# A two-layer graph network: the order of the node strips and where the nodes are prepared

## The chip, the cores and the metric

The kernel runs on one NeuronCore of a Trainium2 chip. The metric is device time in microseconds (us) of one execution; several executions of the same kernel are given by their median. Engines are called by their names in the trace: PE (TensorE), DVE (VectorE), ACT (ScalarE), POOL (GpSimd) and SP (the queue that issues most DMAs). Nodes lie in 26 blocks of 128 (3,327 nodes and one of padding).

## What is computed

Two residual layers over 3,327 nodes with 64 features and a dense 0/1 adjacency matrix of 3,327 x 3,327. Layer 0 sums, for every pair of nodes, an attention weight times a hyperbolic logarithm map; layer 1 is a weighted sum in which the weight halves with each later neighbour. Cut to what matters:

```python
h = jnp.maximum(_layernorm(x, axis=-1), 0.0)
# layer 0, on h
c = 1.0 / r[0] ** 2
x_t = logmap0(h, c)                       # needs artanh of the norm, so logarithms
left, right = x_t @ w_att[:D, 0], x_t @ w_att[D:, 0]
adj_att = sigmoid(left[:, None] + right[None, :] + b_att[0]) * adj
x_local = logmap(h[:, None, :], h[None, :, :], c)        # for every pair i, j
support = jnp.einsum('ij,ijd->id', adj_att, x_local)
x = x + proj(expmap(h, support, c), c)
# layer 1
h = jnp.maximum(_layernorm(x, axis=-1), 0.0)
support = h @ weight
rank = jnp.cumsum(adj != 0, axis=1); deg = rank[:, -1:]
k = jnp.minimum(deg, 100.0); pos = rank - (deg - k)
w = (adj != 0) * jnp.where(pos > 0, 0.5 ** (k - pos), 0.0)
x = x + w @ support + bias
```

## The kernel before

**Pairs and rounds.** The nodes i are cut into four strips of 8, 8, 6 and 4 blocks (`STRIPS`, line 29). For each strip the kernel goes through all 26 blocks j from the last to the first. A round is one such j (two j in the last strip, where two tiles of 512 columns lie side by side): 26 rounds for each of the first two strips, 26 for the third, 13 for the last. In round n (lines 1145 to 1194) the engines do, on tiles of 128 x 1024:

- DVE, line 1169: the attention weight (a tanh from ACT) times the adjacency tile `ad`. This line opens a round on DVE.
- DVE, line 626 (`edges`): the 0/1 mask of a later round's tile.
- PE, lines 637 and 638 (`count`): how many neighbours lie behind each pair, accumulated in PSUM; it is copied out by `read` (lines 641 to 652), in one round by ACT and in the next by DVE, into `behind_hi`, `weight_of` or `behind_lo`, for layer 1.
- ACT, line 659 (`sigmoids`): the tanh of left + right for the next round.
- PE, lines 666 and 667 (`products`): two matmuls of features, `ju` by `iu` and `jz` by `iz`, that give the pair's function argument in `pq`.
- ACT, lines 1162 and 1163: two Gelus on `pq`, in place.
- DVE, line 1186: `pq` times the weight; PE, line 676 (`total`): the sum over j with the table `hw`, two rounds later.

So a steady round holds on DVE 1169, 626, 1186 and every other time a read; on ACT two Gelus, a tanh and every other time a read. PE, DVE and ACT execute in the order in which the program is written (`manual_schedule`, line 685). SP and POOL take their work in an order that the framework chooses. `ad` has five buffers, `sg` five, `pq` two.

**Preparation, lines 689 to 884.** Before the first round the nodes' features have to be there: `x_sb` is loaded in two halves of 13 blocks, then for all 26 blocks at once: mean and centring (701, 702), squares and relu on ACT (703 to 705), sums (721, 723), a reciprocal root by a guess and three Newton steps on DVE (728), `x2`, `bal`, `babs`, `nrm`, `yz` (730 to 768). The scaled features `zf` are split into an f16 part and an f16 remainder (`nz`), and `nu` holds them with seven columns more. Blocks 0 to 7 (`first_i`) and 24, 25 (`last_j`) are turned by PE first and copied to `jz` and `ju`; four DMAs make from these the strip's `iz` and `iu` (`strip_in`, line 572), two of them issued on POOL for the first strip. Then logarithms for all blocks on ACT, with a table load before (801) and after (815), the artanh on DVE (818 to 822), and `logits`, which multiplies `jz` with the attention vectors into `left` and `right`. `first_left` transposes `left` for the first strip. The blocks 8 to 23 (`later`) follow: zf, rounding, transposes on PE in two groups, the second in `last_of_ahead` (line 853), a generator of which round 0 and round 1 take a piece each (lines 1187 to 1189; those rounds skip `advance`). It also makes `left_d` (left in DRAM, for the later strips), the table `hw`, and some columns for later. The adjacency tiles of rounds 0 and 1 are masked, counted and read before any of this is ready (706, 716 to 719).

**After the strips, lines 1202 to 1277.** Layer 1: the counts are turned into weights (`decode`), alternately by ACT and DVE, and PE adds up over j in the order: the four blocks of `JD` (12 to 15), then the other blocks of the first three strips, then the blocks of the last strip (`late`), whose `s2` is ready last. `close` writes out each 512 nodes.

**Post-processing of a strip** (`post`, line 930) runs during the next strip's rounds in small portions (`advance`), its small operations on POOL; these are the operations of line 982 in the trace, among them powers (`ALU.pow`) on 128 x 8.

## Time and profile before

| | us |
|---|---|
| median of 3 runs (425.24 to 426.3) | 426.22 |
| the profiled execution, its own time | 425.4 |
| its span, first to last instruction | 423.7 |
| busy: PE / DVE / ACT / POOL | 361.3 / 377.9 / 364.6 / 114.0 |

The profiled execution's own time is 1.7 us more than its span. In the page the span is cut into 40 slices of 10.6 us, and each digit is the busy share of an engine in tenths. Rows of a timeline give start, duration, engine, line, operation, output and inputs with their shapes, and in brackets how long the engine stood idle before and what released it. The chain of work that ended last consists, for 32% of the span, of DVE work, for 28% of ACT work and for 21% of PE work. The three costliest lines of the rounds on DVE and ACT are

| line | engine, what | count | mean, ns |
|---|---|---|---|
| 1186 | DVE, weight times pq | 91 | 1144 |
| 1169 | DVE, tanh times ad | 91 | 1145 |
| 659 | ACT, tanh | 103 | 978 |
| 1162, 1163 | ACT, Gelus | 90 each | 957, 946 |
| 626 | DVE, mask | 91 | 653 |

### The profile page before, as it was taken

To read this page: it belongs to the slowest core of one execution; us is meant where nothing else is said; L and a number is where in the kernel's file an instruction comes from. 1 tells how busy PE (TensorE), PEld (TensorE's weight loads), DVE (VectorE), ACT (ScalarE), POOL (GpSimd) and SP (SyncE) were. 2 spreads that over 40 slices of the span, in tenths; PEclk is the share of its full clock that TensorE was granted. 3 is DMA by queue.
4 is the path that set the end of the run, shared out by engine and by line. 5 is a ranking of instruction groups with operands and counts; after the bars stand their busy time and mean duration, and the time that the engine had idled before them with its cause. 6 is when DMAs were issued, how large, how long until landed. Compare 5 with 4: busy or idle time off the path is not lost.

```text
span 423.7 us, 4689 instructions
## 1 busy us (share of the span) xinstructions
PE 361.3 (85%) x1437; PEld 155.1 (37%) x1460; DVE 377.9 (89%) x557; ACT 364.6 (86%) x410; POOL 114.0 (27%) x218
## 2 busy tenths in 40 slices
PE   0246779999999899999999799999787999899693
PEld 0024323333333333333333444444332333244353
DVE  4886899999999999999999898899998999898841
ACT  3468859999999999999999999999898899789720
POOL 6010000000000044780061061940523375362400
PEclk9999989999999999999999899999998999999987
DMA  7311544545456535543444454444553430000012
GB/s 184 150 39 39 151 131 124 164 145 177 137 167 183 169 116 159 181 143 112 149 124 148 120 150 122 140 130 132 164 143 105 137 99 0 2 0 0 2 26 63
DMA packets 23248, 48.98 MB, mean 116 GB/s; under 512 B 8713, under 2 KB 9169, under 8 KB 23215
## 3 DMA queue, kind: packets, MB, share of 16 engines
q1 hardware_dynamic: 21087, 47.81, 38.3%
q10 hardware_dynamic: 1808, 0.46, 0.6%
q0 software_dynamic: 320, 0.33, 0.5%
q8 instruction: 13, 0.21, 0.2%
q14 instruction: 20, 0.16, 0.1%
HBM read 46.40 MB, written 0.87 MB: 112 GB/s over the span
## 4 chain that ended last, share of the span: by engine, by line
DVE 32%; ACT 28%; PE 21%; issue 12%; POOL 2%; DMA 2%; SPq 0%; POOLq 0%; DVEq 0%; ACTq 0%
ACT sg L659 9%; DVE sg L1186 8%; ACT pq L1162 8%; PE po L676 8%; DVE sg L1169 7%; DVE wt L1218 3%; ACT pq L1163 3%; ACT behind_lo L648 3%; PE pq L666 2%; DMA ad<-in_adj_t 2%; PE pq L667 2%; DVE behind_lo L652 2%; ACT behind_hi L648 2%; PE pc L638 2%; PE pc L637 2%
## 5 line engine op out<-in xcount | busy, mean ns | idle before, releaser
L676 PE MATMUL po<-sg,hw 128*65 128x512 f32 (+1 forms) x364 | 161.4, 567 | 0.9 <-DVE st L910 0.4
L1186 DVE SCALAR_TENSOR_TENSOR sg<-pq,sg 128x1024 f32<-128x1024 f32 (+1 forms) x91 | 104.1, 1144 | 6.8 <-ACT pq L1163 5.6
L1169 DVE SCALAR_TENSOR_TENSOR sg<-sg,ad 128x1024 f32<-128x1024 f32 (+1 forms) x91 | 104.2, 1145 | 1.6 <-ACT sg L659 1.4
L659 ACT ACTIVATE sg<-left_b,right 128x1024 f32<-128x1024 f32 (+2 forms) x103 | 99.4, 978 | 0.7 <-DVE right L834 0.7
L1162 ACT ACTIVATE pq<-pq 128x1024 f32<-128x1024 f32 (+1 forms) x90 | 86.1, 957 | 4.8 <-PE pq L667 4.6
L1163 ACT ACTIVATE pq<-pq 128x1024 f32<-128x1024 f32 (+1 forms) x90 | 85.2, 946 | 2.8
L676 PEld LDWEIGHTS po<-sg,hw 128*65 128x65 f32 x364 | 49.7, 139 | 71.5 <-issue 56.0
L637 PE MATMUL pc<-mask,ca 128*128 128x512 bf16 (+1 forms) x166 | 60.7, 366 | 15.6 <-DVE behind_hi L652 7.0
L638 PE MATMUL pc<-mask,cb 128*128 128x512 bf16 (+1 forms) x172 | 62.4, 372 | 12.9 <-DVE mask L626 10.6
L666 PE MATMUL pq<-iu,ju 71*128 71x512 f16 (+1 forms) x182 | 68.6, 377 | 1.7 <-DMA iu<-ju 0.7
L667 PE MATMUL pq<-iz,jz 128*128 128x512 f16 (+1 forms) x182 | 67.4, 377 | 0.9 <-DMA iz<-jz 0.9
L626 DVE TENSOR_SCALAR mask<-ad 128x1024 bf16<-128x1024 f32 (+1 forms) x91 | 59.5, 653 | 1.5 <-DMA ad<-in_adj_t 1.5
L638 PEld LDWEIGHTS <-cb 128*128 128x128 bf16 x182 | 17.9, 98 | 66.8 <-issue 49.0
L982 POOL TENSOR_TENSOR dots<-dots,ih 128x8 f32<-128x8 f32 (+1 forms) x3 | 2.6, 874 | 137.2 <-DVE dots L1002 137.2
L1230 PE MATMUL pw<-wt,s 128*128 128x512 bf16 (+1 forms) x151 | 33.7, 375 | 4.3 <-DVE s L1087 2.3
L637 PEld LDWEIGHTS <-ca 128*128 128x128 bf16 x175 | 17.4, 99 | 30.1 <-issue 18.4
L648 ACT ACTIVATE behind_hi<-pc 128x1024 uint8<-128x1024 f32 (+2 forms) x24 | 20.7, 863 | 7.0 <-PE pc L638 7.0
L1230 PEld LDWEIGHTS <-s 128*128 128x128 f16 x182 | 18.0, 101 | 23.6 <-issue 4.2
L666 PEld LDWEIGHTS <-ju 71*128 71x128 f16 x182 | 18.1, 99 | 23.3 <-DVE sg L1186 3.8
L667 PEld LDWEIGHTS <-jz 128*128 128x128 f16 x182 | 18.3, 100 | 21.2 <-issue 3.0
L648 ACT ACTIVATE behind_lo<-pc 128x1024 uint8<-128x1024 f32 (+2 forms) x29 | 24.9, 858 | 0.0
L1235 POOL TENSOR_TENSOR x_sb<-x_sb,bias_b 128x256 f32<-128x256 f32 (+1 forms) x6 | 10.0, 1673 | 49.5 <-DVE w L1071 44.0
(298 smaller groups left out, 365.7 us busy)
## 6 DMA issues: line engine op xcount, KB each, us to landing
ad<-in_adj_t SPq DMA_DIRECT2D x65, 512.0 KB, 3.6
ad<-in_adj_t SPq DMA_DIRECT2D x26, 384.0 KB, 3.1
out<-o SPq DMA_DIRECT2D x6, 128.0 KB, 1.9
left_b<-left_d SPq DMA_DIRECT2D x1, 512.0 KB, 4.7
x_sb<-in_x SPq DMA_DIRECT2D x1, 416.0 KB, 5.0
x_sb<-in_x ACTq DMA_DIRECT2D x1, 416.0 KB, 5.7
iz<-jz SPq DMA_DIRECT2D x3, 128.0 KB, 2.4
left_b<-left_d SPq DMA_DIRECT2D x1, 384.0 KB
```

What stands on the lines that cost most here:

```text
L626: V.tensor_scalar(*args, 0.0, None, op0=ALU.not_equal)
L637: T.matmul(S.pc[:, f0:f1], ca, S.before[:, f0:f1], start=False, stop=True, skip_group_check=True)
L638: T.matmul(S.pc[:, f0:f1], cb, now[:, f0:f1], start=S.first, stop=True, skip_group_check=True)
L648: A.activation(kept, S.pc[:, : S.F], AF.Relu, scale=128.0 if j in JD else 1.0)
L659: A.activation(part(n, sg, j), S.left[:, : S.F], AF.Tanh, bias=right[:, j : j + 1], scale=0.5)
L666: T.matmul(part(n, pq, j, f0, f1), ju[:KB, j, :], S.iu[:, f0:f1], start=True, stop=False)
L667: T.matmul(part(n, pq, j, f0, f1), jz[:, j, :], S.iz[:, f0:f1], start=False, stop=True)
L676: T.matmul(S.po[: D + 1, f0:f1], hw[:, j, :], part(n, sg_of[n], j, f0, f1), start=j == NB - 1, stop=j == 0)
L1162: A.activation(pq, pq, AF.Gelu, scale=-WG / QS)
L1163: A.activation(pq, pq, AF.Gelu, scale=WH)
L1169: V.scalar_tensor_tensor(sg, sg, 1.0, ad_of.pop(n)[:, :w], op0=ALU.add, op1=ALU.mult)
L1186: V.scalar_tensor_tensor(sg, pq, WD, sg, op0=ALU.add, op1=ALU.mult)
```

## The change

The strips are taken in the opposite order of nodes: blocks 18 to 25 first, then 10 to 17, 4 to 9, and 0 to 3 last. As j also runs from 25 down, the first strip's eight blocks are the j of its first eight rounds. Only these eight are prepared ahead of the rounds (`first`); the other 18 (`others`) are prepared in pieces by a generator, `second_group`, one piece at the end of each of the rounds 0 to 8.

Parts of this preparation change engine. For the first eight blocks the additional columns of nu and the table `hw` are made by POOL; `iz` and `iu` come from a second, swapped copy of the features (`nz1[:, 1]`, `nu1[:, 1]`) by two transposing DMAs on SP rather than from `jz` and `ju` by four plain ones. For the other 18 all columns of one value per node are made by POOL, with powers for the two roots and the reciprocal, and so is `hw`; `jz` and `ju` come by two transposing DMAs on SP rather than from PE with copies. The logarithms are taken twice, once for each group, with a table load before and after each. `nz2` and `nu2` use the memory of the two squares. `left_d` is written once for the 18 blocks by a DMA. In layer 1 the order of summation and the pieces of the bias follow the new strips.

Of rounds 0 and 1 the masks, counts and reads come later than before. New names that the text below uses: `the_rest` (POOL, eight operations), `clipped` (the argument of the logarithms), `logarithms` (ACT), `artanh` (DVE), `summing_table` (POOL, hw), `root_of` (POOL, a power and four operations).

```diff
-STRIPS = [(0, 8), (8, 8), (16, 6), (22, 4)]
+STRIPS = [(18, 8), (10, 8), (4, 6), (0, 4)]
...
-    node_halves = (slice(0, 13), slice(13, NB))
-    nc.sync.dma_start(x_sb[:, :13], xv[:, :13])
-    nc.scalar.dma_start(x_sb[:, 13:], xv[:, 13:])
+
+    first, others = slice(STRIPS[0][0], NB), slice(0, STRIPS[0][0])
+    n1, n2 = NB - first.start, first.start
+    half = first.start + n1 // 2
+    nc.sync.dma_start(x_sb[:, first.start : half], xv[:, first.start : half])
+    nc.scalar.dma_start(x_sb[:, half:], xv[:, half:])
+    nc.scalar.dma_start(x_sb[:, others], xv[:, others])
...
+        if k == 0:
+            nc.sync.dma_start_transpose(iz, nz1[:, 1].rearrange("p b c d -> p (b c d)"))
+            nc.sync.dma_start_transpose(iu, nu1[:, 1].rearrange("p b f -> p (b f)"))
+        else:
+            nc.sync.dma_start(iz[:D], jz[D:, blocks])
+            nc.sync.dma_start(iz[D:], jz[:D, blocks])
+            nc.sync.dma_start(iu[:D], ju[:D, blocks])
+            nc.sync.dma_start(iu[D:KB], ju[KB : KB + 7, blocks])
...
+    nz1 = pre.tile([P, 2, n1, 2, D], F16, name="nz1")
+    nu1 = pre.tile([P, 2, n1, P], F16, name="nu1")
+    G.memset(nu1[:, :, :, D:], 0.0)
+    G.memset(nu1[:, 0, :, D + 6], -WB * QS)
...
+    def centred(bs):
+        V.tensor_reduce(m[:, bs], x_sb[:, bs], AX.X, ALU.add)
+        V.scalar_tensor_tensor(d[:, bs], wide(m[:, bs], bs.stop - bs.start), -1.0 / D, x_sb[:, bs],
+                               op0=ALU.mult, op1=ALU.add)
+
+    def features(bs):
+        V.tensor_mul(zf[:, bs], rl[:, bs], wide(yz[:, bs], bs.stop - bs.start))
+
+    def the_rest(bs, nuj, nui, at):
+
+        n = bs.stop - bs.start
+        G.tensor_scalar(ms[:, bs], nrm[:, bs], ZS, None, op0=ALU.mult)
+        G.tensor_mul(as_[:, bs], as_[:, bs], nrm[:, bs])
+        G.tensor_copy(nuj[:, :, D : D + 3 : 2], ms[:, bs, None].to_broadcast([P, n, 2]))
+        G.tensor_copy(nuj[:, :, D + 3 : D + 5], as_[:, bs, None].to_broadcast([P, n, 2]))
+        G.tensor_sub(nuj[:, :, D + 1], ms[:, bs], nuj[:, :, D])
+        G.tensor_sub(nuj[:, :, D + 5], as_[:, bs], nuj[:, :, D + 3])
+        G.tensor_copy(nui[:, :, at + 3 : at + 6], nuj[:, :, D : D + 3])
+        G.tensor_copy(nui[:, :, at : at + 3], nuj[:, :, D + 3 : D + 6])
+
+    def summing_table(bs):
+
+        G.tensor_scalar(wn[:, bs], nrm[:, bs], WA / 2, None, op0=ALU.mult)
+        G.tensor_scalar(opx[:, bs], x2[:, bs], c_c, 1.0, op0=ALU.mult, op1=ALU.add)
+        G.tensor_mul(hw[:, bs, D], opx[:, bs], wn[:, bs])
+        G.tensor_mul(wn[:, bs], wn[:, bs], y[:, bs])
+        G.tensor_mul(hw[:, bs, :D], rl[:, bs], wide(wn[:, bs], bs.stop - bs.start))
...
+    def clipped(E, bs):
+        n = bs.stop - bs.start
+        E.tensor_mul(s[:, bs], x2c[:, bs], yr[:, bs])
+        E.tensor_scalar(s[:, bs], s[:, bs], sqc, -2.0, op0=ALU.mult, op1=ALU.mult)
+        E.tensor_scalar(g2[n][:, :n], s[:, bs], -2.0 * S0, -2.0 * SMAX, op0=ALU.min, op1=ALU.max)
+        E.tensor_scalar(s[:, bs], s[:, bs], -2.0 * S0, None, op0=ALU.max)
+
+    def logarithms(bs):
+        n = bs.stop - bs.start
+        A.activation(g[n], g2[n], AF.Ln, bias=one_c, scale=-0.5)
+        A.activation(g2[n], g2[n], AF.Ln, bias=one_c, scale=0.5)
+        A.activation(g3[:, bs], s[:, bs], AF.Square, scale=-0.5)
+        A.activation(g3[:, bs], g3[:, bs], AF.Square, bias=q0_c, scale=Q1)
+        A.activation(load_table, one_c, AF.Gelu)
...
+        plr = ps.tile([P, NB, 2], F32, name=tag, bufs=bufs)
+        for b in range(bs.start, bs.stop):
+            for part in (0, 1):
+                T.matmul(plr[:, b, :], jz[:, b, :], w_h[:, part], start=part == 0, stop=part == 1)
...
+    A.activation(load_table, one_c, AF.Ln)
+    centred(first)
+    A.activation(sq1, d[:, first], AF.Square)
+    A.activation(rl[:, first], d[:, first], AF.Relu)
+    A.activation(sr1, rl[:, first], AF.Square)
...
+    V.tensor_reduce(ss[:, first], sq1, AX.X, ALU.add)
+    V.tensor_scalar(v[:, first], ss[:, first], 1.0 / D, EPS_LN, op0=ALU.mult, op1=ALU.add)
+    guess(V, yt[:, first], y[:, first], v[:, first])
+    newton(V, yt[:, first], y[:, first], v[:, first], 3)
+    V.tensor_reduce(rs[:, first], sr1, AX.X, ALU.add)
+
+    V.tensor_mul(x2[:, first], y[:, first], y[:, first])
+    V.tensor_mul(x2[:, first], x2[:, first], rs[:, first])
+    V.tensor_scalar(bal[:, first], x2[:, first], negc, 1.0, op0=ALU.mult, op1=ALU.add)
+    G.tensor_scalar(as_[:, first], x2[:, first], za_c, None, op0=ALU.mult)
+    V.scalar_tensor_tensor(babs[:, first], bal[:, first], -1.0, bal[:, first], op0=ALU.mult, op1=ALU.max)
+    V.reciprocal(nrm[:, first], babs[:, first])
+    the_rest(first, nu1[:, 0], nu1[:, 1], D)
+    V.scalar_tensor_tensor(yz[:, first], nrm[:, first], zs_c, y[:, first], op0=ALU.mult, op1=ALU.mult)
+    features(first)
+    A.copy(nz1[:, 0, :, 0], zf[:, first])
+    A.copy(nz1[:, 1, :, 1], zf[:, first])
+    V.tensor_copy(nu1[:, :, :, :D], zf[:, None, first].to_broadcast([P, 2, n1, D]))
+    V.tensor_sub(nz1[:, 0, :, 1], zf[:, first], nz1[:, 0, :, 0])
+    A.copy(nz1[:, 1, :, 0], nz1[:, 0, :, 1])
+    strip_in(0)
+    V.tensor_scalar(x2c[:, first], x2[:, first], MIN_NORM, None, op0=ALU.max)
+    guess(V, yt[:, first], yr[:, first], x2c[:, first])
+    newton(V, yt[:, first], yr[:, first], x2c[:, first], 1)
+    pt = ps.tile([P, 16, P], F16, name="pq", bufs=2)
+    for b in range(n1):
+        T.transpose(pt[:, b, :], nz1[:, 0, b].rearrange("p c d -> p (c d)"), id16)
+    A.copy(jz[:, first], pt[:, :n1])
+    pt = ps.tile([P, 16, P], F16, name="pq", bufs=2)
+    for b in range(n1):
+        T.transpose(pt[:, b, :], nu1[:, 0, b], id16)
+    V.tensor_copy(ju[:KB, first], pt[:KB, :n1])
+    newton(V, yt[:, first], yr[:, first], x2c[:, first], 2)
+    clipped(V, first)
+    logarithms(first)
+    edges(0)
+    count(0, NB - 1)
+    read(0, NB - 1)
...
+    artanh(first)
+    logits(first, "po", 1)
     products(0)
+    summing_table(first)
     pl = first_left()
+    edges(1)
+    count(1, NB - 2)
     products(1)
     pq = pq_of[0]
     A.activation(pq, pq, AF.Gelu, scale=-WG / QS)
     A.activation(pq, pq, AF.Gelu, scale=WH)
+    read(1, NB - 2)
+    centred(others)
+    edges(AHEAD)
     strips[0].left, left_b = pl, strips[0].left
     sigmoids(0)
     A.copy(left_b[:, : strips[0].F], pl[:, : strips[0].F])
     strips[0].left = left_b
+    A.activation(sq2, d[:, others], AF.Square)
+
+    def second_group():
+
+        o = others
+        A.activation(rl[:, o], d[:, o], AF.Relu)
+        V.tensor_reduce(ss[:, o], sq2, AX.X, ALU.add)
+        G.tensor_scalar(v[:, o], ss[:, o], 1.0 / D, EPS_LN, op0=ALU.mult, op1=ALU.add)
+        root_of(y[:, o], v[:, o])
+        A.activation(sr2, rl[:, o], AF.Square)
         yield
+        V.tensor_reduce(rs[:, o], sr2, AX.X, ALU.add)
+
+        nz2 = pre.tile([P, n2, D], F32, name="sq2").bitcast(F16).rearrange("p b (c d) -> p b c d", c=2)
+        nu2 = pre.tile([P, n2, D], F32, name="sr2").bitcast(F16)
+        G.memset(nu2[:, :, D:], 0.0)
+        G.memset(nu2[:, :, D + 6], -WB * QS)
+        G.memset(nu2[:, :, KB + 6], 1.0)
+        G.tensor_mul(x2[:, o], y[:, o], y[:, o])
+        G.tensor_mul(x2[:, o], x2[:, o], rs[:, o])
+        G.tensor_scalar(bal[:, o], x2[:, o], negc, 1.0, op0=ALU.mult, op1=ALU.add)
+        G.tensor_scalar(yt[:, o], bal[:, o], 0.0, 2.0, op0=ALU.max, op1=ALU.mult)
+        G.tensor_sub(babs[:, o], yt[:, o], bal[:, o])
+        G.tensor_tensor(nrm[:, o], babs[:, o], minus1, op=ALU.pow)
+        G.tensor_mul(yt[:, o], babs[:, o], nrm[:, o])
+        G.tensor_scalar(yt[:, o], yt[:, o], -1.0, 2.0, op0=ALU.mult, op1=ALU.add)
+        G.tensor_mul(nrm[:, o], nrm[:, o], yt[:, o])
+        G.tensor_mul(yz[:, o], nrm[:, o], y[:, o])
+        G.tensor_scalar(yz[:, o], yz[:, o], zs_c, None, op0=ALU.mult)
+        G.tensor_scalar(as_[:, o], x2[:, o], za_c, None, op0=ALU.mult)
+        the_rest(o, nu2, nu2, KB)
+        G.tensor_scalar(x2c[:, o], x2[:, o], MIN_NORM, None, op0=ALU.max)
+        root_of(yr[:, o], x2c[:, o])
+        clipped(G, o)
+        yield
+        yield
+        features(o)
+        A.copy(nz2[:, :, 0], zf[:, o])
+        V.tensor_copy(nu2[:, :, :D], zf[:, o])
+        yield
+        V.tensor_sub(nz2[:, :, 1], zf[:, o], nz2[:, :, 0])
+        nc.sync.dma_start_transpose(ju[:, o], nu2.rearrange("p b f -> p (b f)"))
+        nc.sync.dma_start_transpose(jz[:, o], nz2.rearrange("p b c d -> p b (c d)"))
+        summing_table(o)
+        yield
+        A.activation(load_table, one_c, AF.Ln)
+        logarithms(o)
+        yield
+        artanh(o)
+        logits(o, "pq", 2)
+        nc.sync.dma_start(left_d.rearrange("(b p) -> p b", p=P)[:, o], left[:, o])
+        yield
+        V.tensor_scalar(ih, babs, 2 / WA, None, op0=ALU.mult)
...
+    def root_of(y, v):
+
+        t = yt[:, others]
+        G.tensor_tensor(y, v, nhalf, op=ALU.pow)
+        G.tensor_mul(t, y, y)
+        G.tensor_mul(t, t, v)
+        G.tensor_scalar(t, t, -0.5, 1.5, op0=ALU.mult, op1=ALU.add)
+        G.tensor_mul(y, y, t)
...
-        if n < 2:
-            next(rest_of_ahead)
+        if next(rest_of_ahead, True) is None:
...
-    late = STRIPS[-1][0]
-    order = [*JD, *range(JD.start), *range(JD.stop, late)]
+    late = range(STRIPS[-1][0], STRIPS[-1][0] + STRIPS[-1][1])
+    order = [*JD, *(j for b0, nb in STRIPS[:-1] for j in range(b0, b0 + nb) if j not in JD)]
```

## The prediction

> **What bounds the kernel now.** I read the page first (busy tenths, chain), then the timelines of VectorE, ScalarE and GpSimd over the first 82 us, then stretches of 10 us, then the tail. The page's slices:
>
> ```profile
> DVE  4886899999999999999999898899998999898841
> ACT  3468859999999999999999999999898899789720
> POOL 6010000000000044780061061940523375362400
> ```
>
> VectorE and ScalarE are full from the seventh slice (64 us) on; ahead of it lie holes on both. The stretches give VectorE 4.06, 8.03, 8.88, 5.76, 8.59, 9.83 and 9.74 us busy in the first seven tens: 54.9 of 70, so 15.1 idle. GpSimd does nothing there from 8.4 to 150 us but two copies and two DMA issues. Now VectorE's timeline:
>
> ```profile
> 5.87 1.02 DVE L701 TENSOR_REDUCE m<-x_sb 128x13 f32<-128x832 f32 x1 [5.87 <-DMA x_sb<-in_x]
> 20.88 0.32 DVE L735 RECIPROCAL nrm<-babs 128x26 f32<-128x26 f32 x1
> ...
> 38.60 1.23 DVE L1169 SCALAR_TENSOR_TENSOR sg<-sg,ad 128x1024 f32<-128x1024 f32 x1 [1.12 <-ACT sg L659]
> 39.74 0.69 DVE L626 TENSOR_SCALAR mask<-ad 128x1024 bf16<-128x1024 f32 x1
> ...
> 74.53 1.22 DVE L1169 SCALAR_TENSOR_TENSOR sg<-sg,ad 128x1024 f32<-128x1024 f32 x1
> ...
> 81.40 1.22 DVE L1169 SCALAR_TENSOR_TENSOR sg<-sg,ad 128x1024 f32<-128x1024 f32 x1
> ```
>
> Line 1169 opens a round: round 0 starts at 38.60, round 8 at 74.53, round 10 at 81.40. Two steady rounds take 6.87 us, so eight cost 27.5; these took 35.9, with 8.4 us of remaining preparation and waits among them. What follows round 12 (three more strips, tail) has the same shapes in the new kernel. I therefore compare the start of round 8, and what is still owed then.
>
> GpSimd, in strip 0's later steps, beside full rounds:
>
> ```profile
> 163.21 0.20 POOL L982 TENSOR_TENSOR rn<-rn,rt 128x8 f32<-128x8 f32 x1
> ...
> 171.13 1.23 POOL L982 TENSOR_SCALAR k<-k,absr 128x8 f32<-128x8 f32 x1 [6.30 <-ACT k L1024]
> ...
> 178.12 1.67 POOL L982 TENSOR_TENSOR y<-t,minus 128x8 f32<-128x8 f32 x1
> ```
>
> The same small operation takes 0.20 or 1.2 us; a power of 8 columns takes 1.67 (2.72 at 159.56). From 171.13 to 190.41 are 35 operations, 2 of them powers: 19.3 - 3.5 = 15.8 us for 33, or 0.48 each, where unhindered ones step by 0.28.
>
> **What the Trainium skill says.** "GPSIMD Engine Reference", section Specifications: GpSimd's SBUF interface is shared with VectorE and contends with instructions in a two-port mode or with two SBUF inputs. The trace fits: the long ones are about one L1169 (1.13) longer, and L1169 has two SBUF inputs. "DMA: Bandwidth & Descriptors", section Latency and other measured facts, gives transposing DMAs 261 GB/s; "VectorE: DVE Perf Modes", section The three transpose paths, gives 1309 ns for one 128x128 through DMA. This trace has none: these are my two ends. "ScalarE: Activation LUTs", section What ACT_TABLE_LOAD costs: 1283 ns and a drain of 1380; the trace shows 1.28 (27.82, 30.35) and ScalarE going on after it, so I take 1.28 + 0.2.
>
> **Part 1, the head, with 8 blocks (estimates scaled from rows of before).** The 256 KB of the first blocks land at 4.0 (416 KB per queue took 5.0 from an issue at 0.80). Mean and centring, 8/13 of 0.95 each: 5.2. The reciprocal of r waits for a DMA issued at 1.32 that takes 5.6: 6.9. Eight scalar operations 0.7, a sum 0.6, twelve steps of the root at 0.2, a sum 0.6, and 1.1 to nrm: 12.4, against 21.2 before. GpSimd's eight operations on nu1 start there, among two-input VectorE work, and end at 16.7 (14.7 unhindered, 8 x 0.28). VectorE meanwhile makes zf and both copies, to 15; ScalarE's last half of nz1 is ready at 15.4. TensorE's eight transposes of nu1 (1.05) and the copy to ju (0.5) end at 18.4; six steps of the root and four of clipping, which stand behind that copy on VectorE, at 20.5. Logarithms 1.1, artanh 1.2, left and right 0.5, with edges(0) between: 23. Eight transposes of left (1.9), while ScalarE has a table load (1.5), read(0), two Gelus (1.95) and read(1): sigmoids(0) at 28.2, round 0 at 29.2. Gain: 9.4 us. iz and iu are issued at 15.4 and 16.8 and used at about 22: at 261 GB/s, 256 KB each need 1 us and some 2 of latency (left_b<-left_d and iz<-jz landed in 2.4 to 4.7). Hidden; at 1.31 per block they end after 26, costing 5.
>
> **Part 2, what goes into the rounds.** VectorE gets centring of 18 blocks 2.6, two sums 2.6, zf 1.25, a copy 0.9, the remainder 1.3, artanh and logits 1.7: 10.4. It loses the last ju copy 0.6, left_t 0.3, logits of the 16 blocks 0.4 and the hw table (wn, opx, 1.03 + 0.93, four small) 2.8: 4.1. Net +6.3. ScalarE gets three squares and relu 3.7, a copy 1.25, logarithms 1.15, two table loads 3.0, less a jz copy 0.9: +8.2. Two engines full in rounds can't hide this, but before's 8.4 us excess in rounds 0 to 8 shrinks by its own idle (about 2).
>
> **Part 3, the waits on GpSimd.** GpSimd starts on the 18 blocks at 34.7, when ss is summed. A power of 18 columns: 6 columns took 1.35 at best, 8 took 1.67, so 0.16 per column, 3.3; with no hindrance and no other cost 2.0 might be the floor, 5 the ceiling. To yz stand 2 powers, about 15 small operations and 3 memsets (1.3): 6.6 + 15 x 0.28 + 1.3 = 12.1 unhindered, 46.8; at 0.48 each, and with the waits for rs (38.3), 51.4. I take 51.4 because VectorE's two-input work (L1169, edges, centring) fills half a round. Features(others) stands at the end of round 3. Rounds 0 to 3 start at 29.2, 34.6, 39.3 and 43.4: VectorE has 1.13 + 0.60 + 1.13 in each, a read of 1.22 in every other, the sums of 1.3 at the ends of rounds 0 and 1, and in round 0 sq2 on ScalarE (1.25) ahead of the next sigmoid, on which counts and reads then wait. So features is reached at 46.3. So VectorE waits 5.1; behind it are L1169 of round 4 and all edges. ScalarE stands too, at nz2's copy, 45.7 to 52.7, with round 4's Gelus behind. Then GpSimd does 9 operations to nu2 (61.3), a power and 9 more to the clipped argument: 67.1 (unhindered 57). Rounds 4, 5 and 6 start at 53.7 (after zf and its copy), 59.0 (after the remainder) and 61.9. Logarithms(others), in round 5, is reached on ScalarE at 62.4: ScalarE waits 4.7, then 1.15 and the Gelu load 1.5, and only then round 6's Gelus: VectorE waits at L1186 from 64.8 to 71.8. The transposing DMAs, issued on SP at 61.3 with the next loads of ad behind them, land by 67 (590 KB each, 2.3 us at the page's rate, with latency); logits need them at 73. Hidden; load(9) behind them comes late by some 5 us, inside the ScalarE wait. left_d of 18 blocks goes out in round 6 in 2,304 pieces of 4 bytes; the second half of x_sb went as 1,808 packets in 0.6% of sixteen engines' span (page, part 3: 0.006 x 423.7 x 16 / 1808 = 22 ns each), so 2304 x 22 / 16 = 3.2 us, or twice that if such small ones are slower; ad's five buffers (four rounds, 13 us) cover it. logits also takes a buffer of pq, so products(8) waits for L1186 of round 7: about 1 us.
>
> Sum: round 8 at 78.4 against 74.53, +3.9. Still owed then: the last small columns 0.75 and the range steps 4 x 0.3, already done by that point before: +2.0. The tail, with the late strip now blocks 0 to 3, wants their x_sb at close(0) (409.1), while the bias is in at 396.5: nothing. hw of 18 blocks on GpSimd (128x256 took 1.59, so some 7) is done at 74, wanted in round 10: nothing. 425.4 + 5.9 = 431.3; the median shown is 0.8 above the profiled execution. I say 431.
>
> **Rivals.** *GpSimd arrives in time.* For: its unhindered sums (46.8, 57) lie at the two points of use, and while VectorE waits nothing hinders it. Against: 0.48 in the rows above. Without both waits round 8 starts near 68: 425.4 - 6.5 + 2 = 421; with a faster head 418.
> *Transposing DMAs are slow.* For: the 1309 ns. At 1.31 per block the head loses 5, and jz of 18 blocks comes 24 us after 66: 90, against 78, +12 or so: 431 + 5 + 13 = 449. This decides on the slower side from some 0.7 us per block. Against: 261 GB/s.
> *No transfer into the rounds works as written* (SP's or GpSimd's queue ordered so that ad loads stand behind the transposes for longer, edges starving): 440.
>
> **How the numbers follow.** GpSimd's waits 0.55 (own range 426 to 438), in time 0.30 (416 to 424.5), slow DMAs 0.12, bad order 0.03. Leaving out most of the slow DMAs and the lowest of the second gives 418 to 442. Within 0.3% (1.3 us, what a measurement can tell from no change) lie 0.06 of the first and 0.02 of the second case. Faster 0.28, same 0.08, slower 0.64.
>
> **What would show it.** Round 0 near 29 (part 1); idle VectorE ahead of zf of the second group and idle ScalarE ahead of its Ln, both released by GpSimd (part 3); table loads of 1.28 in round 5; transposes landing in 3 to 6 us. Wrong if GpSimd's powers of 18 columns take 2 us, if the DMAs take over 10, or if round 0 starts after 34.

## The result, and the profile after

| | before | after |
|---|---|---|
| median, us (range, runs) | 426.26 (425.24 to 427.01, 4) | 438.32 (437.06 to 439.58, 4) |
| profiled execution, its own time | 425.4 | 437.27 |
| its span | 423.7 | 434.7 |

The ratio is 1.0285, its 95% interval 1.0241 to 1.0329: the changed kernel is 12 us slower. Slower was forecast, but with +5.9 between the profiled executions; measured are 437.27 - 425.4 = +11.9. The starts of rounds on VectorE (line 1169 before, line 1206 after) show where they come from:

| round | before | forecast | after | after less before |
|---|---|---|---|---|
| 0 | 38.60 | 29.2 | 28.95 | -9.65 |
| 4 | 59.93 | 53.7 | 57.04 | -2.89 |
| 8 | 74.53 | 78.4 | 76.83 | +2.30 |
| 9 | 78.53 | | 83.99 | +5.46 |
| 12 | 88.27 | 94.1 | 98.78 | +10.51 |
| 26 | 136.34 | | 146.86 | +10.52 |
| 30 | 153.17 | | 165.34 | +12.17 |
| 90 | 362.29 | | 374.53 | +12.24 |

The 94.1 at round 12 is the forecast's 78.4, before's 13.74 from round 8 to 12, and the 2.0 it held still owed. So the head gains what was forecast, round 8 is even 1.6 us ahead of the forecast, and then rounds 8 to 11, where the forecast had 2.0 still owed, lose 8.2. The first change of strips (rounds 26 to 29) adds 1.7, the tail gives 1.2 back, and the time outside the span is 0.9 longer.

The page's slices of the changed kernel, each 10.9 us, in tenths of busy time:

```profile
DVE  3889198679999979999999999889999899898861
ACT  3399188869999989999999989999988799789630
POOL 7407990100000006395024025480240647172400
```

GpSimd is now busy in the first two slices and in the fourth to sixth. VectorE has one hole in the fifth slice (1: 43.5 to 54) and a second, shallower one in the seventh to ninth (8, 6, 7: 65 to 98). The second is the one that the forecast doesn't have. VectorE's timeline of the changed kernel (start, duration, line, operation, and in brackets the idle time before it with what ended it):

```profile
8.30 0.17 DVE L778 RECIPROCAL inv_r<-r_c 128x1 f32<-128x1 f32 x1 [3.21 <-DMA r_c<-in_r]
...
28.95 1.23 DVE L1206 SCALAR_TENSOR_TENSOR sg<-sg,ad 128x1024 f32<-128x1024 f32 x1 [1.37 <-ACT sg L655]
...
54.89 1.36 DVE L718 TENSOR_TENSOR d<-rl,yz 128x1152 f32<-128x1152 f32 x1 [9.37 <-POOL yz L873]
...
57.04 1.24 DVE L1206 SCALAR_TENSOR_TENSOR sg<-sg,ad 128x1024 f32<-128x1024 f32 x1
...
76.83 1.22 DVE L1206 SCALAR_TENSOR_TENSOR sg<-sg,ad 128x1024 f32<-128x1024 f32 x1
...
80.66 1.23 DVE L646 TENSOR_SCALAR weight_of<-pc 128x1024 uint16<-128x1024 f32 x1 [2.02 <-PE pc L634]
...
83.99 1.22 DVE L1206 SCALAR_TENSOR_TENSOR sg<-sg,ad 128x1024 f32<-128x1024 f32 x1
88.36 0.69 DVE L622 TENSOR_SCALAR mask<-ad 128x1024 bf16<-128x1024 f32 x1 [3.15 <-DMA ad<-in_adj_t]
...
90.47 1.22 DVE L1206 SCALAR_TENSOR_TENSOR sg<-sg,ad 128x1024 f32<-128x1024 f32 x1
92.46 0.69 DVE L622 TENSOR_SCALAR mask<-ad 128x1024 bf16<-128x1024 f32 x1 [0.77 <-DMA ad<-in_adj_t]
```

Three things are to be read here: 9.37 us of idle time ahead of the second group's features (line 718), released by GpSimd; a wait for TensorE in round 8; and, from round 9 on, waits for the adjacency tile `ad`, which comes by a plain load that no line of the diff touches. What the loads wait for is on SP, which issues them. Its timeline in the same kernel, up to 100 us:

```profile
73.01 0.39 SPq L895 DMA_DIRECT2D left_d<-left  x1
74.49 2.00 SPq L616 DMA_DIRECT2D ad<-in_adj_t  x1
86.28 0.33 SPq L588 DMA_DIRECT2D left_b<-left_d  x1
86.66 10.55 SPq L616 DMA_DIRECT2D ad<-in_adj_t  x4
```

and, of its waits between 0 and 120 us, the one that matters here (line, what it waits for: us in total, times, longest):

```profile
SPq L588 <- DMA left_d<-left: 9.7, 1, 9.7
```

`left_d` is issued at 73.01. One load of `ad` is issued behind it. Then comes `left_b` of the next strip, which reads `left_d` back and so waits for its landing: SP stands 9.7 us, to 86.28, and the next loads of `ad` are issued from 86.66 only. The one load that went out between is slow too; the chain of waits from 60 to 105 us has it as

```profile
74.49 13.84 DMA ad<-in_adj_t
```

where the median load takes 3.6 us (page, part 6). The stretches of 10 us of the changed kernel (stretch; us; busy time and instruction count of PE, PE's weight loads, DVE, ACT, POOL; granted PE clock; busy share of the DMA engines; GB/s) say why:

```profile
70.00:80.00 10.00, 8.05 (x54) 3.40 (x56) 7.85 (x19) 7.28 (x8) 1.12 (x1) 0.83 0.94 142
80.00:90.00 10.00, 7.62 (x27) 2.81 (x26) 6.11 (x13) 8.12 (x9) 0.00 (x0) 1.00 0.83 92
```

and of the kernel before:

```profile
70.00:80.00 10.00, 10.00 (x37) 3.88 (x36) 10.00 (x11) 9.90 (x11) 0.00 (x0) 1.00 0.51 156
80.00:90.00 10.00, 9.95 (x35) 3.76 (x35) 10.00 (x11) 9.90 (x11) 0.00 (x0) 1.00 0.52 157
```

Before, the DMA engines move 156 GB/s in half of their time. After, they are busy for 0.94 and 0.83 of it and move less. In stretches of 5 us it is clearer: from 75 to 80 us they are busy for 0.94 and move 30 GB/s, while in the first experiment below, where `left_d` goes out in long rows and all else stays, the same stretch has 0.77 at 237 GB/s. They work on `left_d`, 9 KB in pieces of 4 bytes.

### The profile page after: what moved, and what is told of

Read it like the earlier page. It is cut to its first block, busy times and chain, and to the rows that moved or that the text cites. A ratio compares the mean times of both kernels' runs of the same rounds, so it can differ in the third digit from the quotient of the medians.

```text
span 434.7 us, 4666 instructions
## 1 busy us (share of the span) xinstructions
PE 362.4 (83%) x1400; PEld 151.8 (35%) x1423; DVE 375.0 (86%) x541; ACT 364.6 (84%) x412; POOL 149.3 (34%) x276
## 2 busy tenths in 40 slices
DMA packets 32139, 50.27 MB, mean 116 GB/s; under 512 B 17765, under 2 KB 18195, under 8 KB 32106
## 4 chain that ended last, share of the span: by engine, by line
DVE 29%; ACT 27%; PE 17%; issue 11%; POOL 8%; DMA 6%; POOLq 0%; DVEq 0%; ACTq 0%
ACT sg L655 8%; DVE sg L1223 8%; ACT pq L1199 7%; PE po L672 7%; DVE sg L1206 6%; DMA ad<-in_adj_t 4%; ACT pq L1200 4%; DVE wt L1254 3%; ACT behind_lo L644 3%; DVE behind_lo L648 2%; PE pq L662 2%; PE pq L663 2%; ACT behind_hi L644 2%; PE pc L633 2%; PE pc L634 2%
## 5 line engine op out<-in xcount | busy, mean ns | idle before, releaser
L672 PE MATMUL po<-sg,hw 128*65 128x512 f32 (+1 forms) x364 | 166.2, 581 | 0.5 <-DVE st L947 0.4
L633 PE MATMUL pc<-mask,ca 128*128 128x512 bf16 (+1 forms) x168 | 61.9, 369 | 26.3 <-DVE behind_hi L648 18.6
L672 PEld LDWEIGHTS po<-sg,hw 128*65 128x65 f32 x364 | 50.9, 142 | 73.5 <-issue 59.9
L1266 PE MATMUL pw<-wt,s 128*128 128x512 bf16 (+1 forms) x151 | 32.3, 363 | 4.1 <-DVE s L1124 2.2
L663 PEld LDWEIGHTS <-jz 128*128 128x128 f16 x182 | 18.4, 101 | 19.9 <-issue 3.7
```

Of the source, the lines that this page charges most:

```text
L633: T.matmul(S.pc[:, f0:f1], ca, S.before[:, f0:f1], start=False, stop=True, skip_group_check=True)
L663: T.matmul(part(n, pq, j, f0, f1), jz[:, j, :], S.iz[:, f0:f1], start=False, stop=True)
L672: T.matmul(S.po[: D + 1, f0:f1], hw[:, j, :], part(n, sg_of[n], j, f0, f1), start=j == NB - 1, stop=j == 0)
```

## The experiments

Theories. P (pieces): `left_d` in 2,304 pieces keeps the queue and the DMA engines for some 13 us, and the edges starve. G (GpSimd): the wait ahead of the features is the loss. T (TensorE): `logits` and the buffer of `pq` that it takes make round 8 late. The transposing DMAs, the forecast's main rival, are not among them, because they landed in 3.3 and 4.6 us (`iu` and `jz`). TensorE's granted clock isn't among them either; the end of this section comes to it. Each experiment starts from the changed kernel unless it says otherwise, and runs with the kernel before beside it (425.69 in the first four, 426.24 in the next four, 425.75 in the last three).

**First four: one suspect each.** *left in rows.* `left` of the 18 blocks is turned by TensorE into the free part of the logits' PSUM tile, copied by VectorE and sent in 18 rows of 512 bytes; `logits` returns its tile:

```diff
...
-        logits(o, "pq", 2)
-        nc.sync.dma_start(left_d.rearrange("(b p) -> p b", p=P)[:, o], left[:, o])
+        plt = logits(o, "pq", 2)[: o.stop, 512 : 512 + P]
+        T.transpose(plt, left[:, o], ident)
+        V.tensor_copy(left_t, plt)
+        nc.sync.dma_start(left_d.rearrange("(b p) -> b p", p=P)[o], left_t)
```

> left of the 18 blocks is turned on TensorE, copied by VectorE and written to DRAM in 18 rows of 512 bytes; all else as in the changed kernel, the transposing DMAs too. If the 2,304 pieces of 4 bytes of left_d hold up the ad loads (one took 13.8 us to land, and SP stood 9.7 us at left_b), rounds 9 to 12 fall back to steady ones: round 12 some 8 us earlier than 98.8, the time about 430. If the transposing DMAs are what fills the DMA engines from 60 us on, the load of 74.49 still comes late and the time stays within 2 us of 438.

Measured: 435.95 us, ratio 1.0250 (1.0228 to 1.0272). The waits for `ad` are gone and rounds 9 to 11 take 10.69 us where the changed kernel takes 14.79: 4.1 less. Round 8 still takes 7.2. So of the 8.2 us that rounds 8 to 11 lose in the changed kernel, 4.1 go with the pieces, 3.2 lie in round 8 (7.16 where before it took 4.00), and 0.9 stay in rounds 9 to 11 (10.69 where before they took 9.74). In the median the rows are worth 2.4 us, and the interval overlaps that of the changed kernel, so by time alone it wouldn't be shown.

*One more buffer of pq,* left unused, taken after the logits:

```diff
+        ps.tile([P, FMAX], F32, name="pq", bufs=2)
```

> One unused buffer of pq is taken after logits of the second group, so that the products of round 8 take the buffer that round 6 left and need not wait for round 7's line 1223. If that wait costs what rounds 8 and 9 lose (2.0 us of VectorE at weight_of, 2.6 of ScalarE), round 9 comes 2 to 3 us earlier; the time falls by as much only if the late ad loads do not take it back, so 436 to 438. If the late loads decide alone, 438.

Measured: 439.38, 1.0333 (1.0286 to 1.0380). No gain. Round 8 opens at 76.77 and round 9 at 84.37, and the wait for TensorE ahead of `weight_of` is still there with 2.45 us. Which of the two buffers `products(8)` finds isn't what counts.

*GpSimd in program order.* In the trace GpSimd works on `yr`'s power at 45.73, ahead of the reciprocal's power at 49.25 on which `yz` waits, although the program has them the other way round:

```profile
35.61 3.58 POOL L917 TENSOR_TENSOR y<-v,nhalf 128x18 f32<-128x18 f32 x1
...
45.73 3.25 POOL L917 TENSOR_TENSOR yr<-x2c,nhalf 128x18 f32<-128x18 f32 x1
...
49.25 3.22 POOL L868 TENSOR_TENSOR nrm<-babs,minus 128x18 f32<-128x18 f32 x1
...
54.52 0.34 POOL L873 TENSOR_SCALAR yz<-yz,zs_c 128x18 f32<-128x18 f32 x1
...
65.44 0.27 POOL L745 TENSOR_SCALAR s<-s 128x18 f32<-128x18 f32 x1
```

The edit puts GpSimd among the engines that keep the written order:

```diff
-    pairs.enter_context(tc.manual_schedule(engines=IN_ORDER))
+    pairs.enter_context(tc.manual_schedule(engines=IN_ORDER | {mybir.EngineType.Pool}))
```

> GpSimd executes in the order of the program, so the power for yr, the columns for later and hw come behind yz. If the order that the framework chose cost VectorE the 4 us by which its wait of 9.4 exceeds the forecast 5.1, yz is ready 4 to 5 us earlier and that wait falls to about 5; the clipped argument then comes later than 65.7 and ScalarE waits ahead of its logarithms by 0 to 4. The time falls by 0 to 4 us. If GpSimd's order is of no account, the wait stays at 9.

Measured: 436.77, 1.0278 (1.0246 to 1.0310). VectorE's and ScalarE's timelines of this kernel now have

```profile
49.53 1.36 DVE L718 TENSOR_TENSOR d<-rl,yz 128x1152 f32<-128x1152 f32 x1 [4.78 <-POOL yz L873]
```

```profile
62.09 0.31 ACT L749 ACTIVATE g<-g,one_c 128x19 f32<-128x19 f32 x1 [1.58 <-POOL g L744]
```

The wait at the features is half of what it was, and one at the logarithms, which the changed kernel doesn't have, appears beside it. Round 4 comes 5.4 us earlier (51.60), round 8 3.6 (73.21), and by round 12 (95.16) `ad` is late again. The profiled execution (433.91) keeps these 3.6 us; in the median it is 1.6, and the interval overlaps that of the changed kernel.

*The chain on VectorE.* `y`, `x2`, `bal`, `babs`, `nrm`, `yz` of the 18 blocks go from GpSimd to VectorE, in the form that the first eight blocks have:

```diff
...
-        G.tensor_tensor(nrm[:, o], babs[:, o], minus1, op=ALU.pow)
...
-        G.tensor_scalar(yz[:, o], yz[:, o], zs_c, None, op0=ALU.mult)
+        V.reciprocal(nrm[:, o], babs[:, o])
+        V.scalar_tensor_tensor(yz[:, o], nrm[:, o], zs_c, y[:, o], op0=ALU.mult, op1=ALU.mult)
```

> The root y, x2, bal, babs, nrm and yz of the 18 blocks are worked out by VectorE (18 more small operations of 0.2 us, some 4 us), GpSimd keeps the rest. If GpSimd's chain is what VectorE waits for, the wait of 9.4 ahead of zf vanishes and round 4 comes 5 to 6 us earlier; the time falls by as much unless the late ad loads further on take it back, so about 432. If the rounds' own work decides, the 4 us are added and the time is 440 or more.

Measured: 434.63, 1.0231 (1.0177 to 1.0285). No wait ahead of the features; round 8 opens at 73.77, but round 12 at 97.20, with a wait of 4.08 for `ad`. The median is 3.7 us below that of the changed kernel, and the intervals overlap. So neither P nor G removed alone gives a gain that is clear of the noise, and in each of these kernels the other loss is still there.

**Next four: both together, and the pieces in the kernel before.** *Mixed.* GpSimd in program order keeps `y` and all that comes after `yz`; six instructions from `x2` to `yz` are VectorE's, one round later:

```diff
-    pairs.enter_context(tc.manual_schedule(engines=IN_ORDER))
+    pairs.enter_context(tc.manual_schedule(engines=IN_ORDER | {mybir.EngineType.Pool}))
...
-        G.tensor_mul(x2[:, o], y[:, o], y[:, o])
...
-        G.tensor_scalar(yz[:, o], yz[:, o], zs_c, None, op0=ALU.mult)
+        yield
+        V.tensor_mul(x2[:, o], y[:, o], y[:, o])
...
+        V.reciprocal(nrm[:, o], babs[:, o])
+        V.scalar_tensor_tensor(yz[:, o], nrm[:, o], zs_c, y[:, o], op0=ALU.mult, op1=ALU.mult)
...
         yield
-        yield
         features(o)
```

> GpSimd in program order keeps the root y; VectorE works out x2, bal, babs, nrm and yz of the 18 blocks in round 2's piece (six operations, 1.4 us), so that one of GpSimd's three powers and some eight operations go. If waits on GpSimd are what the rounds lose before round 5, VectorE's wait ahead of zf vanishes, round 4 starts near 48 (57.0 in the changed kernel), and the logarithms' argument is there in time. left_d still goes out in pieces of 4 bytes: rounds 9 to 11 then lose more than before, as they come earlier and the load behind left_d lands no earlier against them; the time is 431 to 434. If rounds 0 to 5 are filled by work and not by waits, round 4 starts at 54 or later.

Measured: 433.66, 1.0174 (1.0138 to 1.0211); this interval lies clear of the changed kernel's. No wait at the features, round 4 at 49.42 and round 8 at 69.34, 7.5 us ahead of the changed kernel. But the four rounds from 8 to 12 then take 26.4 us (95.78), one load of `ad` lands after 16.8 us, and VectorE waits 4.85 and 2.27 us for it.

*Mixed, with left in rows* (the edit of the first experiment on top):

> As e6_mixed, with left_d in rows as in e1_left_rows. If the wait on GpSimd and the pieces of left_d are the two main losses and add up, 4 us better than e6_mixed and 8 or 9 better than the changed kernel: 427 to 430. If what is lost at one place is only taken back at the next (PE's clock, ScalarE's table loads), within 3 us of e1_left_rows: 433 to 436.

Measured: 425.44, 0.9990 (0.9967 to 1.0013), no difference from before. Against the kernel that differs by the pieces alone it is 433.66 - 425.44 = 8.2 us faster, and the trace has most of it: rounds 8 to 11 take 18.9 us and not 26.4, and no load of `ad` takes more than 4.2. What is left in round 8 is on TensorE. TensorE's and VectorE's timelines of this kernel:

```profile
63.18 1.10 PE L770 MATMUL pq<-w_h,jz 128*128 128x2 f16 x36 [4.40 <-DVE sg L1223]
```

```profile
61.81 1.22 DVE L1223 SCALAR_TENSOR_TENSOR sg<-pq,sg 128x1024 f32<-128x1024 f32 x1 [2.20 <-ACT pq L1200]
...
73.76 1.23 DVE L647 TENSOR_SCALAR weight_of<-pc 128x1024 uint16<-128x1024 f32 x1 [3.10 <-PE pc L635]
```

The logits stand on TensorE for the buffer of `pq` that line 1223 reads, 4.40 us, with the sum and the counts of the coming rounds behind them, and VectorE waits 3.10 us for those counts later.

*The same with one more buffer of pq:*

> As e7_mixed_rows, with the unused buffer of pq of e2_pq_turn. With the late loads gone, the wait of round 8's products for round 7 could now show: 1 to 3 us less than e7_mixed_rows if it does, no difference if TensorE is late there for another reason.

Measured: 425.69, 0.9994 (0.9977 to 1.0010). No difference again. TensorE still stands 4.4 us at the logits; the additional buffer is taken only behind them.

*Only the pieces, in the kernel before.* There `left` of 26 blocks is turned by TensorE and sent in rows; here it goes out in 3,328 pieces, and nothing else of the change is in:

```diff
-        plt = ps.tile([P, P], F32, name="po")
-        T.transpose(plt[:NB, :], left, ident)
-        V.tensor_copy(left_t, plt[:NB, :])
-        nc.sync.dma_start(left_d.rearrange("(b p) -> b p", p=P), left_t)
+        nc.sync.dma_start(left_d.rearrange("(b p) -> p b", p=P), left)
```

> The kernel before with one part of the change alone: left_d goes out by a DMA of 4-byte pieces, 3,328 of them for 26 blocks, in place of a transpose on TensorE, a copy and rows. If the pieces cost what the changed kernel shows (left_b stood 9.7 us behind 2,304 of them), left_b stands some 14 us, an ad load lands late and the time rises by 3 to 8 us. If ad's five buffers cover it, as the forecast had it, the time stays within 1 us of the kernel before.

Measured: 435.78, 1.0227 (1.0193 to 1.0261), +9.5 us from one line that takes work from two engines. Its VectorE timeline, its SP timeline and SP's waits from 30 to 110 us:

```profile
67.65 0.69 DVE L623 TENSOR_SCALAR mask<-ad 128x1024 bf16<-128x1024 f32 x1 [10.20 <-DMA ad<-in_adj_t]
```

```profile
44.68 0.39 SPq L598 DMA_DIRECT2D left_d<-left  x1
...
60.90 0.35 SPq L587 DMA_DIRECT2D left_b<-left_d  x1
```

```profile
SPq L587 <- DMA left_d<-left: 14.2, 1, 14.2
```

The load that ends VectorE's wait, in the chain of waits from 60 to 105 us:

```profile
61.34 6.29 DMA ad<-in_adj_t
```

As in the changed kernel `left_b` stands for `left_d` and the loads stand behind it. Here no load of `ad` goes out between the two, so this is the stand alone: the load is issued 0.4 us after `left_b`, and the mask comes 10.20 us late. Round 3 opens at 56.23, as before (56.69), and round 4 at 69.76 instead of 59.93.

**Last three: which part of the DMA it is, and what is left.** *Pieces on GpSimd's queue.* In the mixed kernel `left_d` and the next strip's `left_b` are issued by GpSimd; the pieces stay:

```diff
-            nc.sync.dma_start(S.left[:, : S.F], bass.AP(...
+            (nc.gpsimd if k == 1 else nc.sync).dma_start(S.left[:, : S.F], bass.AP(...
...
-        nc.sync.dma_start(left_d.rearrange("(b p) -> p b", p=P)[:, o], left[:, o])
+        nc.gpsimd.dma_start(left_d.rearrange("(b p) -> p b", p=P)[:, o], left[:, o])
```

> As e6_mixed (433.7), with left_d still in 2,304 pieces of 4 bytes, but this DMA and the left_b that reads it are issued by GpSimd, which has nothing else to do then. If the ad loads came late because they stand behind the pieces, and behind left_b's wait, on SP's queue, they come in time and the time is that of e7_mixed_rows, 425 to 427. If the pieces keep the DMA engines themselves from the ad loads, it stays at 431 to 434.

Measured: 427.58, 1.0047 (1.0032 to 1.0062). The part of the page on DMA issues (KB, median us from issue to landing) and GpSimd's waits from 50 to 110 us:

```profile
left_d<-left POOLq DMA_DIRECT2D x1, 9.0 KB, 14.1
```

```profile
POOL left_b L588 <- DMA left_d<-left: 13.2, 1, 13.2
```

The transfer is as slow as before, but now it is GpSimd that stands for it, and nothing of the rounds is behind. That brings 433.66 - 427.58 = 6.1 us of the 8.2, or 5.6, as the kernel before was 0.5 us faster beside these runs. The two loads of `ad` that SP issues while the pieces run (from 68.34 us on) still take 12.6 and 10.9 us to land (the one in the mixed kernel took 16.8): the slow landing comes with the pieces on either queue, and what is gone is SP's stand. Of the remaining 2 us (427.58 against 425.44) some 0.8 lie outside the span (2.6 us between time and span, against 1.8); inside it a wait of 2.08 us for `ad` is left.

*Logits in the middle of a round.* Mixed, rows and the additional buffer, with the logits and what follows them moved into round 7, behind its sum on TensorE:

```diff
-        plt = logits(o, "pq", 2)[: o.stop, 512 : 512 + P]
-        T.transpose(plt, left[:, o], ident)
...
+        if n == 7:
+            second_logits()
```

> From e8_mixed_rows_turn: only the logits' matmuls move, from the end of round 6 into round 7 behind that round's total, so TensorE needs not stand for round 6's line 1223; but round 7's tanh for round 8 now waits for them. If TensorE's stand is the loss, round 9 comes 2 to 4 us earlier, 422 to 424; if the tanh's wait takes it back, 425 to 426.

Measured: 424.44 (22 runs), 0.9973 (0.9948 to 0.9997). It is the lowest median here, but by 0.3% and with an interval that ends just below 1; against the mixed kernel with rows (425.44) the intervals overlap. Nor is it one value: 12 of the 22 times lie between 421.77 and 424.44, ten between 426.97 and 429.85, none between these groups, and the profiled execution (428.07) is of the upper one. In its trace the edit doesn't do what it was made for: TensorE stands 3.66 us at the logits, still for the multiplication of round 6, and 1.74 at the transpose of `left` behind them.

*The same one round earlier,* with `y` on VectorE so that features, transposes and artanh can each be taken earlier:

```diff
-        root_of(y[:, o], v[:, o])
+        guess(V, yt[:, o], y[:, o], v[:, o])
+        newton(V, yt[:, o], y[:, o], v[:, o], 3)
...
-        artanh(o)
...
+        if n == 6:
+            second_logits()
```

> From e8_mixed_rows_turn: the root y of the 18 blocks goes to VectorE too (12 small operations, 2.4 us), features come in round 2 and the transposing DMAs in round 3, and artanh and logits stand inside round 6, where the buffer of pq has long been free. If TensorE standing at logits for round 6's line 1223 (4.4 us in e7_mixed_rows) is what makes rounds 7 and 8 long, two thirds of the some 9 us that rounds 6 to 8 take too long go: round 9 starts near 72 to 74 and the time is 420 to 423. If the two table loads and the added work of ScalarE decide, round 9 stays near 77 and the time at 425.

Measured: 425.88, 0.9993 (0.9970 to 1.0017). The expected 420 to 423 didn't come. TensorE's stand at the logits falls to 0.76 us (2.06 at the transpose of `left`), and rounds 8 to 11 take 16.9 us, 2.0 less than in the mixed kernel with rows; but rounds 0 to 2, which now hold `y` and the features on VectorE, take 20.0 us instead of 15.0, and round 8 opens at 72.70 instead of 68.83.

**What no run varied: TensorE's clock.** TensorE's timeline in the mixed kernel with rows, and two of its stretches of 2 us (columns as above):

```profile
64.81 3.62 PE L673 MATMUL po<-sg,hw 128*65 128x512 f32 x4
...
70.91 1.88 PE L673 MATMUL po<-sg,hw 128*65 128x512 f32 x4
```

```profile
66.00:68.00 2.00, 2.00 (x3) 0.38 (x2) 2.00 (x3) 0.03 (x1) 0.00 (x0) 0.50 0.35 33
...
72.00:74.00 2.00, 2.00 (x9) 0.76 (x8) 0.24 (x1) 1.97 (x3) 0.00 (x0) 1.00 0.49 201
```

From 64 to 70 us, behind the stand at the logits, the granted clock is 0.50. The four matmuls of a sum take 3.62 us there and 1.88 at 1.00, a matmul of the counts 0.63 and 0.38. So the wait of 3.10 us for the counts holds the slow clock as well as the stand. The changed kernel has 0.50 from 54 to 66 us, behind 11.2 us in which TensorE stood idle, and again from 74 to 76; the last two experiments have it from 66 to 72 and from 64 to 70.

It is also what marks the 1.7 us at the first change of strips. Rounds 26 to 29 take 18.4 to 18.5 us in the traces of the changed kernel and of six experiments (rows alone, GpSimd in order, the chain on VectorE, the pieces in the kernel before, and the last two), and 16.8 in the others and in the kernel before. No edit separates these groups, and TensorE stands idle for 1.7 to 1.9 us there in all of them. Behind that the clock falls to 0.50 or 0.51 in every trace of the first group and stays at 1.00 in every one of the second, as in these stretches of the changed kernel and of the kernel before:

```profile
156.00:158.00 2.00, 2.00 (x5) 0.77 (x4) 2.00 (x4) 2.00 (x4) 0.00 (x0) 0.50 0.34 55
```

```profile
146.00:148.00 2.00, 2.00 (x6) 0.67 (x5) 2.00 (x4) 2.00 (x4) 0.00 (x0) 1.00 0.57 139
```

What decides between the two in an execution is open.

## Why the prediction was right or wrong

**The step that failed.** "`left_d` of 18 blocks goes out in round 6 in 2,304 pieces of 4 bytes … 22 ns each … so 2304 x 22 / 16 = 3.2 us, or twice that if such small ones are slower; ad's five buffers (four rounds, 13 us) cover it." It took 86.28 - 73.01 = 13.3 us. With 2304 / 16 = 144 pieces on each of 16 engines that is 92 ns for a piece, as an estimate with latency and other traffic in it; the same pieces took 82.22 - 65.52 = 16.7 us in the mixed kernel, 116 ns, and the 3,328 in the kernel before 60.90 - 44.68 = 16.2 us, 78 ns. The price of 22 ns came from packets of the load of `x_sb` of some 250 bytes each (page, part 3: 0.46 MB in 1,808), which are no model for single elements. The Trainium skill, "DMA: Bandwidth & Descriptors", section Rules for kernel authors, says that a strided last dimension lowers to one descriptor per element and is to be rearranged; the count in the forecast was right (the page of the changed kernel has 17,765 packets under 512 bytes, that of the rows 15,454), and the runs give the price that the Trainium skill's page doesn't.

And the cover was wrong in kind, not only in size. The forecast held only the transfer against the five buffers. Behind it on SP stands `left_b`, which waits for it to land, and behind `left_b` all further loads of `ad`; and a load that does go out beside the pieces lands late, after 13.84 us. Where the forecast had nothing, this costs 4.1 us in rounds 9 to 11 of the changed kernel, and 8.2 us once GpSimd's wait is gone, of which some 6 come back when another queue takes the two DMAs. The second term that was too small is round 8's: "about 1 us", measured 3.2 (below). Together these are 7.3 of the 8.2 us that rounds 8 to 11 lose.

**Head: right.** Forecast 29.2, measured 28.95. The reciprocal of r was due at 6.9 and ran at 8.30 (its DMA took 6.9 us, the 5.6 of the kernel before was assumed), and the sum came out all the same.

**GpSimd's first wait: right that it comes, wrong in size, and for a reason that wasn't in the working.** Forecast 5.1, measured 9.37. The powers of 18 columns were right (3.3; 3.22 to 3.58). The difference is the order: the framework put `yr`'s power and other operations ahead of `yz`. With the written order the wait is 4.78, close to the forecast.

**GpSimd's second wait: didn't come, and for the same reason.** Forecast 4.7 on ScalarE at the logarithms, with the argument ready at 67.1. It was ready at 65.7 (65.44 + 0.27), and the rounds were later by then. Waits of 9.4 where 9.8 were forecast: the sum held by luck, through two errors of opposite sign. In the written order the second wait does appear, at 1.58.

**Transposing DMAs: right.** Hidden, 3.3 to 4.6 us to land against the forecast's 3 to 6. That is nearer to 261 GB/s (the Trainium skill, "DMA: Bandwidth & Descriptors", section Latency and other measured facts) than to the 1309 ns for one block (the Trainium skill, "VectorE: DVE Perf Modes", section The three transpose paths) times 18 blocks, which would be 23.6 us. The rival of 449 falls.

**hw on GpSimd: hidden as forecast,** with 2.12 us instead of "some 7".

**"products(8) waits for L1186 of round 7: about 1 us": the mechanism near, the size off.** It is the logits themselves that stand on TensorE for the buffer, 3.22 us in the changed kernel and 4.40 in the mixed one with rows, and the counts behind them come late by 2.02 and 3.10. Round 8 takes 7.16 us where the same round took 4.00 before. The forecast had neither this stand nor the clock of 0.50 behind it; the runs don't separate the two.

**Rivals.** "GpSimd arrives in time" said round 8 near 68 and 421 us. The mixed kernel with rows makes both the case: round 8 opens at 68.83, as forecast, and the time is 425.44. From round 8 to 12 it takes 18.9 us where the forecast had 13.74 + 2.0 = 15.7; 3.2 of the 4.4 missing us lie there, where TensorE stands at the logits and then runs at half its clock. The run that moved the logits left a stand of 3.66 us, so how much of the 3.2 is theirs stays open. "Edges starving" behind DMAs on SP's queue, 440 us, was given 0.03 and is close to what happened; only the DMA at the head of the queue was another.

**Shown, and not shown.** Shown by runs whose intervals are clear of each other: the pieces cost 8.2 us with GpSimd's wait gone, and 9.5 alone in the kernel before; GpSimd's wait, with the clock behind it, costs some 4.7 with the pieces in place (changed against mixed); without both the change is worth nothing. Its head is still ahead there: the mixed kernel with rows opens round 0 10.1 us before the kernel before, round 8 5.7 and round 12 0.5. What takes this back is the work that was moved into full rounds and, in round 8, TensorE; how much is whose isn't shown. The losses don't add up from one alone: with the wait of 9.37 in place, rows bring 2.4 us, without it 8.2. In both kernels one load of `ad` goes out between the pieces and SP's stand, in round 7, so the traces show no fuller store of tiles in one of them; what differs in the traces is the transfer, 13.3 us against 16.7, and with it VectorE's waits for `ad`, 3.9 us in all against 7.1. Why the same pieces take longer in the mixed kernel is open, and so is what sets TensorE's clock.

## What to carry to other kernels

Price a DMA by its pieces, not its bytes, and then walk down the queue that issues it: the instruction that reads the result back waits for its landing, and everything behind that on the same queue waits as well, here the loads that feed every round. When two stalls lie near each other, remove both before judging either: here the rows brought 2.4 us beside the other stall and 8.2 without it. Work taken from an idle head and put into rounds where two engines are full is paid for there, and so are the new waits between engines; here the two ate all of a gain of 9.65 us that was real. And look at the granted clock behind every stand of TensorE before putting a late result down to the stand alone.

## What was not expected of the hardware

Single elements of 4 bytes from SBUF to DRAM cost 78 to 116 ns each per DMA engine (estimates, see above), and while they run the engines of the changed kernel show 0.77 to 0.94 busy at 30 to 48 GB/s (75 to 85 us), against 0.51 at 156 in the kernel before. A load of 512 KB that starts beside them takes 11 to 17 us on whichever queue they are, instead of 3.6. A multiply of 128x1152 on GpSimd took 2.12 us, while the addition of 128x256 from which the forecast scaled took 1.59 in the mean. TensorE's granted clock fell to half behind stands of 1.9 us in some executions and not behind stands as long in others. The power of 18 columns took 3.22 to 3.58 us, in line with 1.67 for 8 columns.
